# Two-layer graph attention on one core: feature-major head aggregation, pre-added softmax sums, second scores by dot products, deferred last aggregation

**Chip, cores, metric.** One NeuronCore of one Trainium2 chip. The metric is the device time of the whole program in microseconds (us), median of the timed runs. All runs quoted here agree within about 0.6% for one kernel and count as fast runs. In the profiles PE is TensorE, PEld its loading of stationary operands ("weight loads"), DVE is VectorE, ACT is ScalarE, POOL is GpSimd. The span goes from the first to the last instruction of the profiled run. The granted clock is the share of TensorE's full clock that it had in a stretch; 1.00 is full.

## The reference, cut to what matters

For each of 32 graphs (512 nodes, 512 features): layer norm and relu, a one-head graph attention with residual, then again layer norm and relu and a two-layer graph attention (4 heads of 256 features, then one head of 512).

```python
def gat_layer(x, mask, W, a_src, a_dst, bias, concat):
    xl = (x @ W).reshape(B, N, H, F)
    asrc = jnp.einsum('bnhf,hf->bnh', xl, a_src)
    adst = jnp.einsum('bnhf,hf->bnh', xl, a_dst)
    e = jax.nn.leaky_relu(asrc[:, :, None, :] + adst[:, None, :, :], NEG_SLOPE)
    e = jnp.where(mask[..., None], e, NEG_INF)
    attn = jax.nn.softmax(e, axis=1)
    out = jnp.einsum('bsdh,bshf->bdhf', attn, xl)
    ...                                         # concat or mean, + bias
h = jax.nn.elu(gat_layer(x, mask, W1, ..., concat=True))     # W1: 512 x 1024
h = gat_layer(h, mask, W2, ..., concat=False)                # W2: 1024 x 512
```

All of it is f32.

## The kernel before

T = 4 blocks of 128 nodes, H = 4 heads, F = 256, KH = 8 blocks of hidden features. E[s, d] are the softmax weights before division by their sum. The framework sets each engine's order of instructions when it builds the kernel; an engine then runs its stream in that order.

```python
def edge_weights(E, pq, h, a_of, a2_of, mask):
    p_row = spread(...); q_row = spread(...)            # TensorE: a value per node to a row
    for t in range(T):
        nc.scalar.activation(q, q_row, AF.Identity, bias=a2_of(t), scale=1.0)
        nc.vector.scalar_tensor_tensor(u, p_row, a_of(t), q, op0=ALU.add, op1=ALU.max)
        nc.gpsimd.tensor_add(u, u, mask[:, t, :])
        nc.scalar.activation(E[:, t, :], u, AF.Exp)

def inverse_sums(E):                                    # layer 0 and layer 2
    for t in range(T):
        for s in range(T):
            nc.tensor.matmul(ps[:, t:t+1], E[:, s, node_block(t)], ones, ...)
    nc.vector.reciprocal(r, ps)

def layer1_head(b, h, E):                               # nodes on the partitions
    for t in range(T):                                  # 257 columns: features and a column of ones
        acc = aggregate(E, t, lambda s: xl[:, s, h, :], F + 1)
        nc.vector.reciprocal(r[:, t:t+1], acc[:, F:F+1])
        nc.vector.scalar_tensor_tensor(v[:, t, :], acc[:, :F], r[:, t:t+1], b1_r[...], ...)
    ...                                                 # elu; later 8 transposes of v to h1T

def layer2_scores(b):
    ac, a2 = score_cols(H1T[b], wa2, 2, "2")            # 32 matmuls with 2 columns
    ...

# graph b:
layer1_project(b)
E = layer1_head_scores(b, 0)
for h in range(H):
    if more and h == 1:
        layer0_scores(b + 1); ...
    E_next = layer1_head_scores(b, h + 1) if h + 1 < H else None
    layer1_head(b, h, E); ...
if more: layer0_out(b + 1)
layer2_scores(b); layer2_project(b)
if more: layer1_in(b + 1)
layer2_out(b)
```

## Time and profile before

| | before |
|---|---|
| time, median of 2 | 5198.85 us (5193.39 to 5204.31) |
| span of the profiled run | 5205.4 us |
| TensorE busy / idle | 5003.1 / 202 us |
| granted TensorE clock, mean | 0.931 |
| one graph in the steady part | 160.4 us |

TensorE is the bound. The lines are in the prediction below. In the groups, the first number after the bar is busy time in us and the second the mean duration in ns; matmuls overlap one another, so busy time over count is the price on the line of time.

### The profile page before, as it was taken

To read this page: it belongs to the slowest core of one execution; us is meant where nothing else is said; L and a number is where in the kernel's file an instruction comes from. 1 tells how busy PE (TensorE), PEld (TensorE's weight loads), DVE (VectorE), ACT (ScalarE), POOL (GpSimd) and SP (SyncE) were. 2 spreads that over 40 slices of the span, in tenths; PEclk is the share of its full clock that TensorE was granted. 3 is DMA by queue.
4 is the path that set the end of the run, shared out by engine and by line. 5 is a ranking of instruction groups with operands and counts; after the bars stand their busy time and mean duration, and the time that the engine had idled before them with its cause. 6 is when DMAs were issued, how large, how long until landed. Compare 5 with 4: busy or idle time off the path is not lost.

```text
span 5205.4 us, 52686 instructions
## 1 busy us (share of the span) xinstructions
PE 5003.1 (96%) x20224; PEld 3228.5 (62%) x20224; DVE 2326.8 (45%) x6180; ACT 1794.5 (34%) x2945; POOL 1108.0 (21%) x998
## 2 busy tenths in 40 slices
PE   6999999999999999999999999999999999999999
PEld 3666656666566666666665666656666666666565
DVE  5454434454444544345443444444454434544343
ACT  2333323433224333233332333322433323333232
POOL 1222211222112212122221222211221212222121
PEclk8899999999999999999999999999999999999999
DMA  2000000000000000000000000000000000000000
GB/s 103 20 13 17 25 25 25 9 17 25 25 25 9 17 25 25 25 17 17 17 25 25 25 9 17 25 25 25 9 17 25 25 25 17 17 17 25 9 9 9
DMA packets 53802, 111.11 MB, mean 21 GB/s; under 512 B 1840, under 2 KB 1840, under 8 KB 53552
## 3 DMA queue, kind: packets, MB, share of 16 engines
q1 hardware_dynamic: 50688, 100.67, 5.5%
q10 hardware_dynamic: 2864, 7.08, 0.4%
q8 instruction: 160, 2.62, 0.2%
q14 instruction: 90, 0.74, 0.0%
HBM read 74.19 MB, written 33.55 MB: 21 GB/s over the span
## 4 chain that ended last, share of the span: by engine, by line
PE 86%; POOL 5%; DVE 5%; ACT 3%; issue 1%; DMA 1%; DVEq 0%; POOLq 0%; ACTq 0%; SPq 0%
PE acc L222 31%; PE acc L399 18%; PE acc L333 17%; PE ps_c L309 8%; POOL u L204 5%; PE row L165 4%; PE pt L173 3%; PE ps L212 3%; DVE u L203 3%; ACT q L201 2%; ACT E L205 1%; DVE v L367 1%; DMA x<-in_x_dram 0%; DVE junk L126 0%; DMA adj<-in_adj_dram 0%
## 5 line engine op out<-in xcount | busy, mean ns | idle before, releaser
L222 PE MATMUL acc<-xl,E 128*128 128x257 f32 (+1 forms) x5120 | 1548.6, 453 | 67.2 <-ACT E L205 62.1
L222 PEld LDWEIGHTS acc<-xl,E 128*128 128x128 f32 x5120 | 996.0, 203 | 470.4 <-issue 258.1
L204 POOL TENSOR_TENSOR u<-u,m 128x512 f32<-128x512 f32 x640 | 737.8, 1180 | 1844.2 <-DVE u L203 1803.7
L399 PE MATMUL acc<-w_s,h1T 128*128 128x512 f32 x2048 | 952.9, 619 | 0.0
L333 PE MATMUL acc<-w_s,hT 128*128 128x512 f32 x2048 | 917.3, 604 | 0.0
L203 DVE SCALAR_TENSOR_TENSOR u<-row,ac,q 128x512 f32<-128x512 f32 x640 | 447.5, 745 | 747.5 <-ACT q L201 746.1
L333 PEld LDWEIGHTS acc<-w_s,hT 128*128 128x128 f32 x2048 | 392.1, 196 | 449.8 <-issue 449.8
L399 PEld LDWEIGHTS acc<-w_s,h1T 128*128 128x128 f32 x2048 | 397.9, 201 | 436.7 <-issue 436.7
L201 ACT ACTIVATE q<-row,a 128x512 f32<-128x512 f32 x768 | 478.9, 682 | 535.2 <-PE row L165 428.4
L338 ACT COPY xl<-acc 128x512 f32<-128x512 f32 x256 | 150.1, 586 | 1340.7 <-PE acc L333 1340.7
L205 ACT ACTIVATE E<-u 128x512 f32<-128x512 f32 x768 | 484.2, 630 | 222.2 <-POOL u L204 221.2
L222 PE MATMUL acc<-h,E 128*128 128x512 f32 x1024 | 453.8, 601 | 6.0 <-DVE x L284 6.0
L180 DVE CUSTOM_DVE_ANT_0 junk_m<-m1T,row 128x512 bf16<-128x512 bf16 x640 | 394.4, 683 | 124.9 <-PE row L165 124.9
L309 PEld LDWEIGHTS ps_c<-wa,h1T 128*128 128x128 f32 x2048 | 335.4, 257 | 50.2 <-PE pt L173 34.1
L309 PE MATMUL ps_c<-wa,h1T 128*128 128x2 f32 x2048 | 333.1, 295 | 28.1 <-DVE r L216 28.1
L222 PEld LDWEIGHTS acc<-h,E 128*128 128x128 f32 x1024 | 194.7, 193 | 238.2 <-issue 224.1
L174 ACT COPY h1T<-pt 128x512 f32<-128x512 f32 x256 | 138.8, 581 | 551.3 <-PE pt L173 551.3
L411 DVE SCALAR_TENSOR_TENSOR x<-acc,r,x 128x512 f32<-128x512 f32 x128 | 96.1, 751 | 401.5 <-PE acc L222 401.5
L165 PE MATMUL row<-ident,pq 128*128 128x128 f32 x1536 | 210.6, 277 | 62.7 <-ACT q L201 53.3
L212 PEld LDWEIGHTS ps<-ones,E 128*128 128x128 f32 x2048 | 258.9, 198 | 11.2 <-ACT E L205 5.4
L212 PE MATMUL ps<-ones,E 128*128 128x1 f32 x2048 | 246.6, 246 | 4.4 <-ACT E L205 4.4
L165 PEld LDWEIGHTS row<-ident,pq 128*128 128x128 f32 x1536 | 175.3, 139 | 120.4 <-ACT q L201 71.1
(71 smaller groups left out, 3727.8 us busy)
## 6 DMA issues: line engine op xcount, KB each, us to landing
adj<-in_adj_dram SPq DMA_DIRECT2D x32, 1024.0 KB, 5.1
x<-in_x_dram SPq DMA_DIRECT2D x32, 1024.0 KB, 5.1
out_dram<-x SPq DMA_DIRECT2D x32, 1024.0 KB, 4.2
w_s<-in_L_gnn_W_dram ACTq DMA_DIRECT2D x2, 2048.0 KB, 21.1
b_r<-in_L_gnn_b_dram ACTq DMA_DIRECT2D x1, 512.0 KB, 11.2
a_r<-in_L_gnn_att_src_dram ACTq DMA_DIRECT2D x1, 512.0 KB, 5.4
a_r<-in_L_gnn_att_dst_dram ACTq DMA_DIRECT2D x1, 512.0 KB, 4.0
ws_r<-in_L_gnn_attn_w_src_dram ACTq DMA_DIRECT2D x1, 256.0 KB, 5.2
```

Of the source, the lines that this page charges most:

```text
L165: nc.tensor.transpose(row[:, node_block(t)], col_of(t).to_broadcast([P, P]), ident)
L173: nc.tensor.transpose(pt[:, node_block(t)], src(t, k), identity)
L180: nc.vector.tensor_tensor_reduce(junk, mask[:, t, :], row, 1.0, LOWEST, ALU.add, ALU.max, accum_out=amax[:, t, h : h + 1])
L201: nc.scalar.activation(q, q_row, AF.Identity, bias=a2_of(t), scale=1.0)
L203: nc.vector.scalar_tensor_tensor(u, p_row, a_of(t), q, op0=ALU.add, op1=ALU.max)
L204: nc.gpsimd.tensor_add(u, u, mask[:, t, :])
L205: nc.scalar.activation(E[:, t, :], u, AF.Exp)
L212: nc.tensor.matmul(ps[:, t : t + 1], E[:, s, node_block(t)], ones, start=(s == 0), stop=(s == T - 1))
L222: nc.tensor.matmul(acc[:, :width], E[:, s, node_block(t)], values(s), start=(s == 0), stop=(s == T - 1))
L309: nc.tensor.matmul(ps[:, t, :], src[:, k, node_block(t)], wa[:, k, :], start=(k == 0), stop=(k == kn - 1))
L333: nc.tensor.matmul(acc, hT[:, k, node_block(t)], w1_s[:, k, half * 512 : (half + 1) * 512], start=(k == 0), stop=(k == KD - 1),)
L399: nc.tensor.matmul(acc, h1T[:, k, node_block(t)], w2_s[:, k, :], start=(k == 0), stop=(k == KH - 1))
```

## The change

Its intent is to take work off TensorE: the head's output is made with features on the partitions (8 wide matmuls for 16 narrower ones, and no transposes), the softmax sums are pre-added on GpSimd so that 4 one-column matmuls do for 16, the second scores become dot products on VectorE, and the last aggregation of a graph moves behind the next graph's first projection. Core of the diff, cuts marked:

```diff
-    p_acc = ...(name="p_acc", bufs=2, space=PSUM)      # and p_tr bufs=2
+    p_acc = ...(name="p_acc", bufs=3, space=PSUM)      # and p_tr bufs=1
 ...
     def inverse_sums(E):
+        total = work.tile([P, N], F32, tag="total", name="total", bufs=1)
+        nc.gpsimd.tensor_add(total, E[0], E[1])
+        for e in E[2:]:
+            nc.gpsimd.tensor_add(total, total, e)
         for t in range(T):
-            for s in range(T):
-                nc.tensor.matmul(ps[:, t : t + 1], E[:, s, node_block(t)], ones, ...)
+            nc.tensor.matmul(ps[:, t : t + 1], total[:, node_block(t)], ones, start=True, stop=True)
 ...
     def layer1_head_scores(b: int, h: int):
-        return E
+        r = inverse_sums(E)
+        r_row = work.tile([P, N], F32, tag="r_row", ...)
+        nc.scalar.copy(r_row, spread(lambda t: r[:, t : t + 1]))
+        return E, r_row
 ...
+        for k in range(h * nk, (h + 1) * nk):           # layer1_head: features on the partitions
+            acc = aggregate_T(E, lambda s: xl[:, s, k * P : (k + 1) * P])
+            nc.vector.tensor_mul(v, acc, r_row)
+            nc.scalar.activation(e, v, AF.Exp, bias=bias, scale=1.0)
+            nc.vector.tensor_scalar(e, e, 1.0, -1.0, op0=ALU.min, op1=ALU.add)
+            nc.vector.scalar_tensor_tensor(H1T[b][:, k, :], v, bias, e, op0=ALU.add, op1=ALU.max)
 ...
+            for i in range(2):                          # layer2_project: scores 2
+                nc.vector.scalar_tensor_tensor(junk, xl[:, t, :], 1.0, att2_r[i], ..., accum_out=ac[:, t, i : i + 1])
 ...
-        E = layer1_head_scores(b, 0)
+        head = layer1_head_scores(b, 0)
+        if b:
+            layer2_out(b - 1)
 ...
+        layer2_project(b)
         layer2_scores(b)
-        layer2_project(b)
         if more:
             layer1_in(b + 1)
-        layer2_out(b)
```

More of the change, by code (lines that the diff above doesn't have):

```diff
@@ L71 @@
     cols = ctx.enter_context(tc.tile_pool(name="cols", bufs=2))
-    p_acc = ctx.enter_context(tc.tile_pool(name="p_acc", bufs=2, space=PSUM))
-    p_tr = ctx.enter_context(tc.tile_pool(name="p_tr", bufs=2, space=PSUM))
+    p_acc = ctx.enter_context(tc.tile_pool(name="p_acc", bufs=3, space=PSUM))
+    p_tr = ctx.enter_context(tc.tile_pool(name="p_tr", bufs=1, space=PSUM))
     p_bc = ctx.enter_context(tc.tile_pool(name="p_bc", bufs=3, space=PSUM))
@@ L107 @@
     nc.scalar.dma_start(w1_s, w1.rearrange("(k p) f -> p k f", p=P))
-    b1_r = const.tile([P, HF], F32, name="b1_r")
+    b1_c = const.tile([P, KH], F32, name="b1_c")
     b2_r = const.tile([P, D], F32, name="b2_r")
     wa1 = const.tile([P, KD, NW], F32, name="wa1")
-    wa2 = const.tile([P, KH, 2], F32, name="wa2")
+    att2_r = [const.tile([P, D], F32, name=f"att2_r{i}") for i in range(2)]
     def fold_attention_weights():
         nc.scalar.dma_start(w2_s, w2.rearrange("(k p) f -> p k f", p=P))
-        nc.scalar.dma_start(b1_r, rows(b1, HF))
+        with nc.allow_non_contiguous_dma(reason="one bias per partition"):
+            nc.scalar.dma_start(b1_c, b1.rearrange("(k p) -> p k", p=P))
         nc.scalar.dma_start(b2_r, rows(b2, D))
         for i, (a1, a2) in enumerate(((att_src1, att_src2), (att_dst1, att_dst2))):
-            a_r = work.tile([P, HF], F32, tag="v", name=f"a1_r{i}")
+            nc.scalar.dma_start(att2_r[i], rows(a2, D))
+            a_r = big.tile([P, HF], F32, tag="adj", name=f"a1_r{i}")
             nc.scalar.dma_start(a_r, rows(a1, HF))
@@ L124, in fold_attention_weights @@
                     f = slice(h * F, (h + 1) * F)
-                    junk = work.tile([P, D], F32, tag="junk", name="junk")
+                    junk = work.tile([P, D], BF16, tag="junk", name="junk")
                     nc.vector.scalar_tensor_tensor(
@@ L129, in fold_attention_weights @@
                     )
-            a_r = work.tile([P, D], F32, tag="v", name=f"a2_r{i}")
-            nc.scalar.dma_start(a_r, rows(a2, D))
-            for k in range(KH):
-                junk = work.tile([P, D], F32, tag="junk", name="junk")
-                nc.vector.scalar_tensor_tensor(
-                    junk, w2_s[:, k, :], 1.0, a_r, op0=ALU.mult, op1=ALU.mult,
-                    accum_out=wa2[:, k, i : i + 1],
-                )
     def node_block(t: int) -> slice:
@@ L193, in shifts, with edge_weights @@
         return pq
-    def edge_weights(E, pq, h, a_of, a2_of, mask):
+    def edge_weights(pq, h, a_of, a2_of, mask, name):
+        E = []
         p_row = spread(lambda t: pq[:, 0, t, h : h + 1])
@@ L199, in edge_weights @@
         for t in range(T):
-            q = work.tile([P, N], F32, tag="q", name="q", bufs=3)
-            nc.scalar.activation(q, q_row, AF.Identity, bias=a2_of(t), scale=1.0)
-            u = work.tile([P, N], F32, tag="u", name="u", bufs=4)
-            nc.vector.scalar_tensor_tensor(u, p_row, a_of(t), q, op0=ALU.add, op1=ALU.max)
+            u = work.tile([P, N], F32, tag="u", name="u", bufs=5)
+            nc.scalar.activation(u, q_row, AF.Identity, bias=a2_of(t), scale=1.0)
+            nc.vector.scalar_tensor_tensor(u, p_row, a_of(t), u, op0=ALU.add, op1=ALU.max)
             nc.gpsimd.tensor_add(u, u, mask[:, t, :])
-            nc.scalar.activation(E[:, t, :], u, AF.Exp)
+            e = big.tile([P, N], F32, tag="E", name=f"{name}_{t}", bufs=13)
+            nc.scalar.activation(e, u, AF.Exp)
+            E.append(e)
+        return E
     def inverse_sums(E):
+        total = work.tile([P, N], F32, tag="total", name="total", bufs=1)
+        nc.gpsimd.tensor_add(total, E[0], E[1])
+        for e in E[2:]:
+            nc.gpsimd.tensor_add(total, total, e)
         ps = p_sm.tile([P, T], F32, tag="sm", name="ps")
         for t in range(T):
-            for s in range(T):
-                nc.tensor.matmul(
-                    ps[:, t : t + 1], E[:, s, node_block(t)], ones, start=(s == 0), stop=(s == T - 1)
-                )
+            nc.tensor.matmul(ps[:, t : t + 1], total[:, node_block(t)], ones, start=True, stop=True)
         r = cols.tile([P, T], F32, name="r")
@@ L217, in inverse_sums, with aggregate, aggregate_T @@
         return r
-    def aggregate(E, t, values, width):
+    def aggregate(E, t, values):
         acc = p_acc.tile([P, 512], F32, tag="acc", name="acc")
         for s in range(T):
-            nc.tensor.matmul(
-                acc[:, :width], E[:, s, node_block(t)], values(s), start=(s == 0), stop=(s == T - 1)
-            )
+            nc.tensor.matmul(acc, E[s][:, node_block(t)], values(s), start=(s == 0), stop=(s == T - 1))
+        return acc
+    def aggregate_T(E, values):
+        acc = p_acc.tile([P, N], F32, tag="acc", name="acc_T")
+        for s in range(T):
+            nc.tensor.matmul(acc, values(s), E[s], start=(s == 0), stop=(s == T - 1))
         return acc
@@ L237, in masks @@
         nc.vector.tensor_scalar(m1, a, 0.0, NO_EDGE, op0=ALU.is_le, op1=ALU.mult)
-        d = cols.tile([P, T, P], F32, name="d")
+        d = work.tile([P, T, P], BF16, tag="junk", name="d")
         for t in range(T):
@@ L260, in layer0_scores @@
             for w, s in ((ws_r, c), (wd_r, a)):
-                junk = work.tile([P, D], F32, tag="junk", name="junk")
+                junk = work.tile([P, D], BF16, tag="junk", name="junk")
                 nc.vector.scalar_tensor_tensor(
@@ L272, in layer0_scores @@
         pq = shifts(c, amax, 1, "0")
-        E = big.tile([P, T, N], F32, tag="E0", name=f"E0_{b}")
-        edge_weights(E, pq, 0, lambda t: a[:, t, :], lambda t: a2[:, t, :], m0T)
+        E = edge_weights(pq, 0, lambda t: a[:, t, :], lambda t: a2[:, t, :], m0T, f"E0_{b}")
         L0[b] = (h0, E)
@@ L282, in layer0_out @@
         for t in range(T):
-            acc = aggregate(E, t, lambda s: h0[:, s, :], D)
+            acc = aggregate(E, t, lambda s: h0[:, s, :])
             nc.vector.scalar_tensor_tensor(
@@ L325, in layer1_project @@
         pq = shifts(ac[:, :, H:], amax, H, "1")
-        xl = big.tile([P, T, H, F + 1], F32, tag="xl", name=f"xl_{b}")
-        nc.gpsimd.memset(xl[:, :, :, F : F + 1], 1.0)
+        xl = big.tile([P, T, HF], F32, tag="xl", name=f"xl_{b}")
         for t in range(T):
@@ L336, in layer1_project @@
                     )
-                nh = 512 // F
-                nc.scalar.copy(
-                    xl[:, t, half * nh : (half + 1) * nh, :F], acc.rearrange("p (h f) -> p h f", f=F)
-                )
+                nc.scalar.copy(xl[:, t, half * 512 : (half + 1) * 512], acc)
         L1[b] = (ac, a2, pq, xl)
-    H1T, V1 = {}, {}
+    H1T = {}
     def layer1_head_scores(b: int, h: int):
         ac, a2, pq, _ = L1[b]
-        E = big.tile([P, T, N], F32, tag="E", name=f"E_{b}_{h}", bufs=2)
-        edge_weights(
-            E, pq, h, lambda t: ac[:, t, h : h + 1], lambda t: a2[:, t, h : h + 1], M[b][2]
-        )
-        return E
@@ L353, in layer1_head @@
-    def layer1_head(b: int, h: int, E):
-        xl = L1[b][3]
-        v = work.tile([P, T, F], F32, tag="v", name=f"v_{b}_{h}")
-        r = cols.tile([P, T], F32, name="r1")
-        for t in range(T):
-            acc = aggregate(E, t, lambda s: xl[:, s, h, :], F + 1)
-            nc.vector.reciprocal(r[:, t : t + 1], acc[:, F : F + 1])
-            nc.vector.scalar_tensor_tensor(
-                v[:, t, :], acc[:, :F], r[:, t : t + 1], b1_r[:, h * F : (h + 1) * F], op0=ALU.mult, op1=ALU.add
-            )
-        e = work.tile([P, T, F], F32, tag="e", name=f"e_{b}_{h}", bufs=1)
-        nc.vector.tensor_scalar(e, v, 0.0, None, op0=ALU.min)
-        nc.scalar.activation(e, e, AF.Exp)
-        nc.vector.scalar_tensor_tensor(v, e, -1.0, v, op0=ALU.add, op1=ALU.max)
-        V1[b, h] = v
@@ L370, in layer1_head_T, with layer1_head @@
-    def layer1_head_T(b: int, h: int):
+        E = edge_weights(
+            pq, h, lambda t: ac[:, t, h : h + 1], lambda t: a2[:, t, h : h + 1], M[b][2], f"E_{b}_{h}"
+        )
+        r = inverse_sums(E)
+        r_row = work.tile([P, N], F32, tag="r_row", name=f"r_row_{b}_{h}", bufs=1)
+        nc.scalar.copy(r_row, spread(lambda t: r[:, t : t + 1]))
+        return E, r_row
+    def layer1_head(b: int, h: int, E, r_row):
+        xl = L1[b][3]
         if h == 0:
             H1T[b] = big.tile([P, KH, N], F32, tag="h1T", name=f"h1T_{b}")
-        v = V1.pop((b, h))
@@ L374, in layer1_head_T @@
         nk = F // P
-        transposed(
-            lambda t, k: v[:, t, node_block(k)], H1T[b][:, h * nk : (h + 1) * nk, :], ident, F32
-        )
-    L2 = {}
-    def layer2_scores(b: int):
-        m1, m1T = M.pop(b)[2:]
-        L1.pop(b)
-        ac, a2 = score_cols(H1T[b], wa2, 2, "2")
-        amax = cols.tile([P, T, 1], F32, name="amax2")
-        neighbour_max(amax, 0, m1T, spread(lambda t: ac[:, t, 0:1]))
-        pq = shifts(ac[:, :, 1:2], amax, 1, "2")
-        E = big.tile([P, T, N], F32, tag="E", name=f"E_{b}_{H}", bufs=2)
-        edge_weights(E, pq, 0, lambda t: ac[:, t, 0:1], lambda t: a2[:, t, 0:1], m1)
-        L2[b] = E
+        for k in range(h * nk, (h + 1) * nk):
+            acc = aggregate_T(E, lambda s: xl[:, s, k * P : (k + 1) * P])
+            bias = b1_c[:, k : k + 1]
+            v = work.tile([P, N], F32, tag="v", name="v")
+            nc.vector.tensor_mul(v, acc, r_row)
+            e = work.tile([P, N], F32, tag="e", name="e")
+            nc.scalar.activation(e, v, AF.Exp, bias=bias, scale=1.0)
+            nc.vector.tensor_scalar(e, e, 1.0, -1.0, op0=ALU.min, op1=ALU.add)
+            nc.vector.scalar_tensor_tensor(H1T[b][:, k, :], v, bias, e, op0=ALU.add, op1=ALU.max)
@@ L393, in layer2_project @@
+    L2 = {}
     def layer2_project(b: int):
         h1T = H1T.pop(b)
-        xl = big.tile([P, T, D], F32, tag="xl", name=f"xl2_{b}")
+        xl = big.tile([P, T, D], F32, tag="xl2", name=f"xl2_{b}")
+        ac = cols.tile([P, T, 2], F32, name="ac2")
         for t in range(T):
@@ L402, in layer2_project, with layer2_scores @@
             nc.scalar.copy(xl[:, t, :], acc)
-        L2[b] = (L2[b], xl)
+            for i in range(2):
+                junk = work.tile([P, D], BF16, tag="junk", name="junk")
+                nc.vector.scalar_tensor_tensor(
+                    junk, xl[:, t, :], 1.0, att2_r[i], op0=ALU.mult, op1=ALU.mult, accum_out=ac[:, t, i : i + 1]
+                )
+        L2[b] = (ac, xl)
+    def layer2_scores(b: int):
+        m1, m1T = M.pop(b)[2:]
+        L1.pop(b)
+        ac, xl = L2[b]
+        a2 = cols.tile([P, T, 1], F32, name="a22")
+        nc.vector.tensor_scalar(a2, ac[:, :, 0:1], SLOPE, None, op0=ALU.mult)
+        amax = cols.tile([P, T, 1], F32, name="amax2")
+        neighbour_max(amax, 0, m1T, spread(lambda t: ac[:, t, 0:1]))
+        pq = shifts(ac[:, :, 1:2], amax, 1, "2")
+        E = edge_weights(pq, 0, lambda t: ac[:, t, 0:1], lambda t: a2[:, t, :], m1, f"E2_{b}")
+        L2[b] = (E, inverse_sums(E), xl)
     def layer2_out(b: int):
-        E, xl = L2.pop(b)
+        E, r, xl = L2.pop(b)
         xt = X.pop(b)
-        r = inverse_sums(E)
         for t in range(T):
-            acc = aggregate(E, t, lambda s: xl[:, s, :], D)
+            acc = aggregate(E, t, lambda s: xl[:, s, :])
             nc.vector.scalar_tensor_tensor(
@@ L431 @@
                     load(b + 2)
-            E_next = layer1_head_scores(b, h + 1) if h + 1 < H else None
-            layer1_head(b, h, E)
-            if h:
-                layer1_head_T(b, h - 1)
-            E = E_next
+            ahead = layer1_head_scores(b, h + 1) if h + 1 < H else None
+            layer1_head(b, h, *head)
+            head = ahead
         if more:
             layer0_out(b + 1)
-        layer1_head_T(b, H - 1)
+        layer2_project(b)
         layer2_scores(b)
-        layer2_project(b)
         if more:
             layer1_in(b + 1)
-        layer2_out(b)
+    layer2_out(B - 1)
 _INS = [
```

## The prediction

> **What bounds the kernel now.** I read the page's busy times first, then the chain that ended last, then the groups split by form, then TensorE's timeline of one steady graph, then the busy times by stretch.
>
> ```profile
> PE 5003.1 (96%) x20224; PEld 3228.5 (62%) x20224; DVE 2326.8 (45%) x6180; ACT 1794.5 (34%) x2945; POOL 1108.0 (21%) x998
> PE 86%; POOL 5%; DVE 5%; ACT 3%; issue 1%; DMA 1%; DVEq 0%; POOLq 0%; ACTq 0%; SPq 0%
> ```
>
> TensorE is busy 96% and makes 86% of the chain; no other engine reaches half. Idle time of TensorE is 5205 - 5003 = 202 us, 6 us in each of the 32 graphs. So time can only come from taking TensorE work away. Which work is there, and what does one instruction cost on the line of time (busy time over count, since the mean duration overlaps its neighbours)?
>
> ```profile
> L222 PE MATMUL acc<-xl,E 128*128 128x257 f32 x4096 | 1064.7, 408 | 67.2 <-ACT E L205 62.1 <-DVE v L361 1.7 <-DVE r L360 0.6
> L399 PE MATMUL acc<-w_s,h1T 128*128 128x512 f32 x2048 | 952.9, 619 | 0.0
> L309 PE MATMUL ps_c<-wa,h1T 128*128 128x2 f32 x2048 | 333.1, 295 | 28.1 <-DVE r L216 28.1
> L212 PE MATMUL ps<-ones,E 128*128 128x1 f32 x2048 | 246.6, 246 | 4.4 <-ACT E L205 4.4
> L165 PE MATMUL row<-ident,pq 128*128 128x128 f32 x1536 | 210.6, 277 | 62.7 <-ACT q L201 53.3 <-DVE pq L191 9.1
> L173 PE MATMUL pt<-ident,v 128*128 128x128 f32 x1024 | 137.9, 273 | 0.3 <-DVE v L367 0.3
> L204 POOL TENSOR_TENSOR u<-u,m 128x512 f32<-128x512 f32 x640 | 737.8, 1180 | 1844.2 <-DVE u L203 1803.7 <-DVE r L360 37.3
> ```
>
> The source asks for 32 x 32 matmuls in the second projection and the trace has 2048: each f32 matmul is two instructions, a transpose one. To be seen: the matmuls for the second scores have two columns and still cost 333.1/2048 = 163 ns each, the sums with one column 120 ns, against 465 ns for 512 columns. A narrow matmul pays for loading the 128 stationary columns.
>
> One graph lasts 2798.65 - 2638.25 = 160.4 us (between the same point of two graphs). The timeline around the second scores:
>
> ```profile
> 2757.56 0.73 PE L309 MATMUL ps_c<-wa,h1T 128*128 128x2 f32 x6
> 2758.15 1.11 PE L399 MATMUL acc<-w_s,h1T 128*128 128x512 f32 x2
> 2759.09 8.88 PE L309 MATMUL ps_c<-wa,h1T 128*128 128x2 f32 x52
> 2767.84 2.06 PE L399 MATMUL acc<-w_s,h1T 128*128 128x512 f32 x2
> 2769.69 1.06 PE L165 MATMUL row<-ident,ac 128*128 128x128 f32 x4
> 2770.54 4.20 PE L399 MATMUL acc<-w_s,h1T 128*128 128x512 f32 x8
> 2774.58 1.04 PE L165 MATMUL row<-ident,pq 128*128 128x128 f32 x8
> 2775.45 22.48 PE L399 MATMUL acc<-w_s,h1T 128*128 128x512 f32 x52
> ```
>
> Two things: some 10 us go to the narrow matmuls, and just after them two wide ones take 2.06 us, where 52 later ones take 22.48, so 0.43 us each. The stretches say why (columns: length, busy PE, PEld, DVE, ACT, POOL, granted clock, DMA):
>
> ```profile
> 2757.50:2767.80 10.30, 10.30 (x63) 9.82 (x61) 1.59 (x7) 3.83 (x6) 6.94 (x6) 0.69 0.01 2
> 2767.80:2797.80 30.00, 30.00 (x76) 14.11 (x77) 8.90 (x27) 6.58 (x11) 4.50 (x4) 0.93 0.10 35
> 2852.90:2903.30 50.40, 45.58 (x267) 38.36 (x266) 32.76 (x76) 33.85 (x57) 23.01 (x20) 0.97 0.00 1
> ```
>
> The granted clock falls to 0.69 under the narrow matmuls. The last row is the head stage, the one where the other engines are fullest: DVE 65%, ACT 67%, POOL 46%. Nearly all of TensorE's idle time is there.
>
> **What the Trainium skill says.** (1) "TensorE: Matmul & The Clock Gate", Part 1: the array's clock is halved after a window of about 3.4 us in which it was little used, and a matmul of 512 columns at full clock starts every 215.7 ns. The trace agrees on the clock (0.69, then two matmuls at twice their time); its f32 instruction takes 429 ns, twice the page's bf16 figure, with two instructions to a matmul. (2) "GPSIMD Engine Reference", section 3.1: an addition of two inputs takes about 2.6 cycles an element at 1.2 GHz. For 512 elements that is an estimate of 1109 ns; the trace has 1180 ns, and I use that. (3) The same page's specifications: GpSimd shares its SBUF interface with VectorE. The profile of before shows no clear slowing (1145 to 2141 ns for the mask additions, median 1157), so I add none. (4) "Perfetto Trace Analysis", Identifying the Most-Contended Engine: weight-load busy share judges TensorE better than matmul busy share. Here 62% against 96% says the same as the narrow matmuls: the array is occupied, not full.
>
> **The change part by part, on TensorE, for all 32 graphs.**
> 1. Heads with features on the partitions: per head 16 matmuls of 257 columns become 8 of 512. 4096 instructions at 260 ns (1064.7 us) become 2048. At the mean 455 ns of the four wide groups of today that is 932 us: -133. (In the densest stretch today's take 220 ns each, so a warm machine would give only some 20; most of this 133 is waiting and a cold clock inside the head stage.)
> 2. No more transposes of v, since the head's output comes out transposed: -138.
> 3. Second scores by dot products on VectorE: the 2048 two-column matmuls go: -333. VectorE gets 8 products a graph at the 0.69 + 0.08 us that the same form takes in layer 0: 6 us a graph, during the projection where it is busy 8.9 of 30 us. Hidden.
> 4. Sums pre-added on GpSimd: today 2 sets of 16 one-column matmuls a graph, then 6 sets of 4 (the heads need their own now, as the column of ones went). 2048 to 1536 instructions at 120 ns: -62. GpSimd gets 18 additions of 1.18 us a graph, 21 us.
> 5. The inverse sum must be spread to a row: 16 more transposes a graph, 512 at 137 to 200 ns: +80.
> 6. The clock after the second scores stays up: the second projection costs 952.9 us against 2048 x 0.429 = 879; I take 50 of the 74 us: -50.
> Sum: -133 - 138 - 333 - 62 + 80 - 50 = -636 us. From 5199 that is 4563.
>
> The other engines: GpSimd goes from 34.6 to about 56 us a graph, in the head stage from 23 to some 41 of about 65 us. VectorE: the head's five kinds of work today (reciprocals 79.9, scaling 242.6, minimum 101.8, maximum 157.9 us: 18.2 us a graph) become 8 products, 8 clampings and 8 maxima of 512, about 15; with the dot products it is 3 us more, 75 a graph. ScalarE stays near 56. None becomes the bound of a graph of 140 us.
>
> What is given back: the transposition pool has one PSUM buffer in place of two. The four groups of hn each need about 0.45 us of TensorE and then a copy of 0.59 us and two hand-overs; today the gaps are filled with the last aggregation's sums (the order in the timeline is hn, sums, hn, sums). Now little else is ready between the second projection and the next graph's first, because scores 2 only start when the projection ends: I estimate 3 us a graph, +96. The clock may fall again there (the 8-column scores follow): +15. The last graph has nothing to hide scores 2 behind: 4 dot-product ends, 4 maxima, 4 edge tiles at GpSimd's pace and 3 additions, about 15 us: +15. At the start the 16 products of the folded second weights (0.68 us) go: -10. In the head stage the sum of a head comes 3 x 1.18 = 3.5 us after its last weights; with one head of lead it should be hidden, and the deferred aggregation of 13.7 us fills the wait for head 0 (today 1.63 + 0.37 + 0.41 us idle); I leave these two against each other with 0. So 4563 + 116 = 4679; since the wide matmuls at 429 ns would take a further 50 us off step 1 if the stage ran without holes, I set 4650.
>
> As a check, the floor: 256 wide matmul instructions a graph of 429 ns = 110 us, and 25 us for scores 1, sums, spreads and transposes at today's warm rates: 135 us. With 80 us at the start and 145 for the last graph, 31 x 135 makes 4410. So 4650 holds 7 to 8 us of waiting a graph, against 4.8 to 6 now.
>
> **Rivals.**
> A. GpSimd's chain replaces TensorE in the head stage. Order on an engine is fixed, so if the sums' matmuls stand ahead of an aggregation in TensorE's stream and GpSimd is late, TensorE stops. For: 41 of 65 us of GpSimd in that stage, sums behind masks in one queue, and single buffers for total and the spread row. Against: TensorE's order today is visibly interleaved (transposes of masks between head matmuls), and the lead is a whole head of 7 us. It would add 3.5 us for each of 4 heads, 450 us: about 5100.
> B. Time comes back in full and the holes close: the deferred aggregation fills both the wait for head 0 and the hT gap, clock stays at 1.0: 4450 to 4500.
> C. The thirteen shared tiles for E: layer 0's four stay till the heads are done, so a head may wait for the head before the last to be aggregated. One tile more than today's twelve, freed singly, speaks against it; it would cost 2 to 4 us a graph, 4720 to 4780.
>
> **Range and chances.** Removals are counted instructions at measured prices and are sure within 15%; the waits are the uncertain term, between 3 and 13 us a graph. Predicted 4650 us, 8 in 10 between 4490 and 4820. Rival A in full still gives 2% less than today, so faster by over 2% is 0.95, within 2% 0.03, slower 0.02.
>
> **What would show it.** Right: no two-column matmuls and no transposes of v; head aggregation 2048 instructions near 910 to 930 us; the first matmuls of the second projection at 0.43 to 0.5 us; a graph of 140 to 145 us; a gap of about 3 us at the hn transposes released by ScalarE's copies; GpSimd near 1790 us. Wrong: TensorE idle over 400 us with releasers GpSimd or the sums' reciprocal (A); idle before edge weights released by TensorE through tile reuse (C); wide matmuls slower than 0.47 us each through the whole stage, which would be a lower granted clock.

## The result, and the profile after

The changed kernel takes 5832.51 us (5832.09 to 5832.94), the ratio to before is 1.1222 with a 95% interval of 1.1201 to 1.1243: 12% slower, where 11% faster was predicted. Ratios are the mean time of one kernel's fast runs over that of the other's of the same rounds, so not quite the ratio of the medians.

The page of the changed kernel: busy times, then the chain that ended last, by engine and by line.

```profile
PE 4989.9 (86%) x15104; PEld 2662.6 (46%) x15104; DVE 2741.3 (47%) x6244; ACT 1797.2 (31%) x2945; POOL 1894.2 (32%) x1542
...
PE 65%; POOL 22%; ACT 5%; issue 4%; DVE 3%; DMA 0%; DVEq 0%; ACTq 0%; POOLq 0%; SPq 0%
PE acc L380 15%; PE acc L221 13%; PE acc L334 12%; POOL u L198 12%; POOL total L209 8%; PE acc_T L228 8%; PE row L159 6%; PE ps L212 5%; PE ps_c L312 4%; DVE u L197 3%; ACT u L196 2%; PE pt L167 2%; POOL total L207 2%; ACT E L200 1%; ACT h L153 1%
```

TensorE has 5120 instructions fewer than before and is still busy 4990 us, as against 5003. It now idles 5830 - 4990 = 840 us in place of 202. In the chain GpSimd has 22% where it had 5%; it waits behind masks (L198) and additions of sums (L209, L207). The groups:

```profile
L228 PE MATMUL acc_T<-E,xl 128*128 128x512 f32 x2048 | 1164.0, 703 | 175.3 <-ACT E L200 175.2
L334 PE MATMUL acc<-w_s,hT 128*128 128x512 f32 x2048 | 1001.1, 634 | 0.0
...
L209 POOL TENSOR_TENSOR total<-total,E 128x512 f32<-128x512 f32 x384 | 560.1, 1458 | 19.0 <-ACT E L200 1.5
...
L212 PE MATMUL ps<-ones,total 128*128 128x1 f32 x1536 | 298.7, 316 | 569.9 <-POOL total L209 569.8
...
L312 PE MATMUL ps_c<-wa,hT 128*128 128x8 f32 x1024 | 215.9, 353 | 0.0
```

Two things are to be read. 570 us of TensorE's idle time stand ahead of the sums' matmuls, released by GpSimd's total, and 175 us ahead of the aggregations, released by edge weights (E). And wide matmuls have become dearer: 2048 instructions of one shape cost 1164 us in the heads and 1001 us in the first projection (917 before), where 2048 x 0.429 us = 879 us would do. Even the 8-column matmuls that the change does not touch went from 119.5 to 215.9 us. TensorE's timeline shows both things in one place (columns: start, length, engine, line, what, count, and the idle time before it):

```profile
2617.09 1.04 PE L159 MATMUL row<-ident,pq 128*128 128x128 f32 x8
2617.97 6.17 PE L221 MATMUL acc<-xl,E 128*128 128x512 f32 x14
2628.07 1.81 PE L212 MATMUL ps<-ones,total 128*128 128x1 f32 x8 [3.93 <-POOL total L209]
2629.74 2.05 PE L221 MATMUL acc<-xl,E 128*128 128x512 f32 x2
2631.59 1.06 PE L159 MATMUL row<-ident,r 128*128 128x128 f32 x4
2632.44 8.30 PE L221 MATMUL acc<-xl,E 128*128 128x512 f32 x16
```

The score rows of head 0 are done at 2617.97. Only 14 wide instructions (6.2 us, the last aggregation that was moved here) follow them in the stream, then the sums' matmuls. These need GpSimd's total, which comes at 2628.07. TensorE idles 3.93 us, and thereafter two wide instructions take 2.05 us, twice the usual. GpSimd in the same time:

```profile
2619.72 3.39 POOL L198 TENSOR_TENSOR u<-u,m 128x512 f32<-128x512 f32 x3 [34.60 <-DVE u L197]
2623.07 1.27 POOL L207 TENSOR_TENSOR total<-E,E 128x512 f32<-128x512 f32 x1
2624.30 1.15 POOL L198 TENSOR_TENSOR u<-u,m 128x512 f32<-128x512 f32 x1
2625.41 2.60 POOL L209 TENSOR_TENSOR total<-total,E 128x512 f32<-128x512 f32 x2
```

Seven operations one behind the other, 8.4 us, on top of a ScalarE and a VectorE step: the chain from rows to total lasts 10.1 us. The stretches tell the rest (length, busy time of PE, PEld, DVE, ACT, POOL, granted clock, DMA), of the changed kernel and, in the last line, of the 8-column matmuls in the kernel before:

```profile
2617.10:2624.10 7.00, 7.00 (x23) 3.34 (x21) 3.47 (x5) 4.91 (x8) 4.38 (x4) 1.00 0.29 111
2624.10:2628.10 4.00, 0.07 (x2) 0.03 (x1) 0.00 (x0) 0.63 (x1) 3.83 (x4) 1.00 0.00 0
2628.10:2632.40 4.30, 4.30 (x14) 3.16 (x15) 0.75 (x2) 0.00 (x0) 0.00 (x0) 0.51 0.00 0
...
2769.60:2776.30 6.70, 6.70 (x33) 6.66 (x32) 0.00 (x0) 0.59 (x1) 0.00 (x0) 0.50 0.00 0
...
2617.97:2798.87 180.90, 155.82 (x475) 83.41 (x473) 85.26 (x193) 56.10 (x92) 59.17 (x48) 0.86 0.05 17
```

```profile
2658.00:2661.50 3.50, 3.50 (x33) 3.43 (x31) 0.75 (x1) 0.00 (x0) 0.13 (x1) 1.00 0.44 167
```

The clock is at 1.00 up to the wait and at 0.51 after it. In the fourth row, the 32 untouched 8-column matmuls after layer 2's sums run at 0.50, 207 ns each (6.63 us for 32 in the chain), where before they ran at 1.00 and 108 ns (3.47 us for 32). The fifth row is one whole graph: 180.9 us at a mean clock of 0.86. Such a wait comes five times a graph (3.93, 3.64, 3.74 and 3.00 us for the heads, 4.09 us for layer 2), and besides one of 5.4 us for head 2's weights.

### The profile page after: what moved, and what is told of

It is laid out like the page before. It is cut to its first block, busy times and chain, and to the rows that moved or that the text cites. A ratio compares the mean times of both kernels' runs of the same rounds, so it can differ in the third digit from the quotient of the medians.

```text
span 5830.3 us, 43175 instructions
## 1 busy us (share of the span) xinstructions
PE 4989.9 (86%) x15104; PEld 2662.6 (46%) x15104; DVE 2741.3 (47%) x6244; ACT 1797.2 (31%) x2945; POOL 1894.2 (32%) x1542
## 4 chain that ended last, share of the span: by engine, by line
PE 65%; POOL 22%; ACT 5%; issue 4%; DVE 3%; DMA 0%; DVEq 0%; ACTq 0%; POOLq 0%; SPq 0%
PE acc L380 15%; PE acc L221 13%; PE acc L334 12%; POOL u L198 12%; POOL total L209 8%; PE acc_T L228 8%; PE row L159 6%; PE ps L212 5%; PE ps_c L312 4%; DVE u L197 3%; ACT u L196 2%; PE pt L167 2%; POOL total L207 2%; ACT E L200 1%; ACT h L153 1%
## 5 line engine op out<-in xcount | busy, mean ns | idle before, releaser
L198 POOL TENSOR_TENSOR u<-u,m 128x512 f32<-128x512 f32 x640 | 729.3, 1159 | 2734.8 <-DVE u L197 2734.8
L228 PE MATMUL acc_T<-E,xl 128*128 128x512 f32 x2048 | 1164.0, 703 | 175.3 <-ACT E L200 175.2
L380 PE MATMUL acc<-w_s,h1T 128*128 128x512 f32 x2048 | 884.1, 592 | 0.0
L212 PE MATMUL ps<-ones,total 128*128 128x1 f32 x1536 | 298.7, 316 | 569.9 <-POOL total L209 569.8
L197 DVE SCALAR_TENSOR_TENSOR u<-row,ac,u 128x512 f32<-128x512 f32 x640 | 442.1, 745 | 494.0 <-ACT u L196 493.2
L228 PEld LDWEIGHTS acc_T<-E,xl 128*128 128x128 f32 x2048 | 418.6, 226 | 531.1 <-issue 289.8
L212 PEld LDWEIGHTS ps<-ones,total 128*128 128x128 f32 x1536 | 288.1, 279 | 739.6 <-POOL total L209 724.8
L196 ACT ACTIVATE u<-row,a 128x512 f32<-128x512 f32 x768 | 471.3, 688 | 315.1 <-PE row L159 315.1
L209 POOL TENSOR_TENSOR total<-total,E 128x512 f32<-128x512 f32 x384 | 560.1, 1458 | 19.0 <-ACT E L200 1.5
L221 PE MATMUL acc<-xl,E 128*128 128x512 f32 x1024 | 527.4, 667 | 4.1 <-ACT E L200 4.1
L367 DVE TENSOR_SCALAR e<-e 128x512 f32<-128x512 f32 x256 | 226.1, 883 | 280.9 <-ACT e L366 280.9
L221 PEld LDWEIGHTS acc<-xl,E 128*128 128x128 f32 x1024 | 212.0, 217 | 230.0 <-issue 223.6
L198 POOL TENSOR_TENSOR u<-u,m0T 128x512 f32<-128x512 f32 x128 | 144.6, 1162 | 493.2 <-DVE u L197 493.2
```

What stands on the lines that cost most here:

```text
L196: nc.scalar.activation(u, q_row, AF.Identity, bias=a2_of(t), scale=1.0)
L197: nc.vector.scalar_tensor_tensor(u, p_row, a_of(t), u, op0=ALU.add, op1=ALU.max)
L209: nc.gpsimd.tensor_add(total, total, e)
L212: nc.tensor.matmul(ps[:, t : t + 1], total[:, node_block(t)], ones, start=True, stop=True)
L221: nc.tensor.matmul(acc, E[s][:, node_block(t)], values(s), start=(s == 0), stop=(s == T - 1))
L228: nc.tensor.matmul(acc, values(s), E[s], start=(s == 0), stop=(s == T - 1))
```

## The experiments

**Theory A**: TensorE's fixed stream has the sums' matmuls some 7 us behind the score rows, GpSimd's chain takes 10 us, so TensorE stands still; what is lost is a matter of placing, not of GpSimd's throughput. **Rival B**: GpSimd's work is itself the bound of the head stage. **Theory D**: a good part of the loss isn't the wait but the halved clock after it. Further rivals stand with the runs; the letters of this section are not those of the prediction. All runs gave a correct result unless said.

**1. Sums behind the aggregation.** The same instructions, written in another order:

```diff
-        r = inverse_sums(E)              # in layer1_head_scores, with r_row
-        return E, r_row
+        return (E,)
 ...                                      # in layer1_head:
+        accs = [aggregate_T(E, lambda s: xl[:, s, k * P : (k + 1) * P]) for k in ks]
+        r = inverse_sums(E)
+        r_row = ...; nc.scalar.copy(r_row, spread(...))
+        for k, acc in zip(ks, accs): ...
 ...                                      # in layer2_out:
+            if t == 0:
+                r = inverse_sums(E)
```

> The changed kernel with the sums (GpSimd additions, the four narrow matmuls, reciprocal, spread row) written after the head's aggregation instead of before it; same instructions. Theory A (TensorE stands still because the sums' matmuls lie only some 7 us of work behind the score rows in its fixed stream while GpSimd's chain takes 10 us, and the clock then halves): five stalls of 3.7 us and about 3 us of half clock after each go, 33 us of 181 a graph, so 4700 to 4900 us, clock 0.93 or more. Rival B (GpSimd and the supply of edge weights are the bound, the place of the sums doesn't matter): the idle time moves to the wait for edge weights, 5500 us or more, clock stays near 0.86.

Measured: 4878.17 us, ratio to before 0.9387 (0.9359 to 0.9415), clock 0.95. Theory A holds, rival B falls: GpSimd does 1844 us of work as against 1894, and the kernel is 954 us faster. TensorE's stream in one graph:

```profile
2501.28 1.04 PE L159 MATMUL row<-ident,pq 128*128 128x128 f32 x8
2502.15 3.60 PE L221 MATMUL acc<-xl,E 128*128 128x512 f32 x8
2505.59 0.95 PE L212 MATMUL ps<-ones,total 128*128 128x1 f32 x8
2506.40 10.55 PE L221 MATMUL acc<-xl,E 128*128 128x512 f32 x24
...
2544.92 2.08 PE L228 MATMUL acc_T<-E,xl 128*128 128x512 f32 x2 [3.72 <-ACT E L200]
```

The heads' and layer 2's sums now follow without idle time and the wide matmuls keep their 0.43 us; only layer 0's sums, which were not moved, still wait 1.9 us a graph. What is left besides is one large wait of 3.7 us for head 2's weights. This first mending beats the kernel before.

**2. Nobody waits for the total.** One operand:

```diff
-            nc.tensor.matmul(ps[:, t : t + 1], total[:, node_block(t)], ones, start=True, stop=True)
+            nc.tensor.matmul(ps[:, t : t + 1], E[t][:, node_block(t)], ones, start=True, stop=True)
```

> The changed kernel with the sums' matmuls reading the four weight tiles' diagonal blocks instead of the pre-added total (wrong result on purpose); the additions on GpSimd still run and nobody waits for them. Theory A: waits shrink to those for the weights and come in pieces of about 1 us, clock 0.93 or more, 4750 to 5050 us. Rival B: GpSimd does the same work, so 5500 us or more.

Measured: 5186.68 us, clock 0.926. Its output is wrong, which doesn't matter for the time. GpSimd's work is unchanged and 646 us go, so rival B falls again. It is over the top of what was expected of theory A: the large wait for head 2's weights (5.4 us) stays, and so do the 8-column matmuls at half clock. The stall is broken into pieces:

```profile
2502.78 3.60 PE L221 MATMUL acc<-xl,E 128*128 128x512 f32 x8
2506.40 0.38 PE L212 MATMUL ps<-ones,E 128*128 128x1 f32 x2
2506.64 1.10 PE L221 MATMUL acc<-xl,E 128*128 128x512 f32 x2
2507.58 0.31 PE L212 MATMUL ps<-ones,E 128*128 128x1 f32 x2
2508.63 0.38 PE L212 MATMUL ps<-ones,E 128*128 128x1 f32 x2 [0.73 <-ACT E L200]
```

Each sum waits for its own tile, 1.0 us at most for this head, and the wide matmuls between keep 1.10 us a pair.

**3. Pre-adding undone.** The sums as 16 one-column matmuls from the weights, in all six sets:

```diff
-        total = ...; nc.gpsimd.tensor_add(...)
-            nc.tensor.matmul(ps[:, t : t + 1], total[:, node_block(t)], ones, start=True, stop=True)
+            for s in range(T):
+                nc.tensor.matmul(ps[:, t : t + 1], E[s][:, node_block(t)], ones, ...)
```

> The changed kernel with the pre-adding undone: 16 narrow matmuls a set straight from the weights, six sets a graph. TensorE gets 12 x 8 x 0.11 = 16 us... worked out: 6 sets x 12 more matmuls x 2 instructions x 0.11 us = 16 us a graph more. Theory A: the stalls break into short waits for single weight tiles, the clock stays up, 33 us saved and 16 us spent: 5200 to 5400 us, faster than the changed kernel although TensorE does more. Rival C (the narrow matmuls themselves are what lowers the clock): slower than the changed kernel, over 5900 us.

Measured: 6021.83 us, clock 0.852. The expectation of theory A was wrong here, and the rival in the expectation had the sign. (Its 12 x 8 x 0.11 is a slip; the sum after it, 16 us, holds.) TensorE is busy 94% of the span: its idle time fell from 840 to 368 us, and its busy time rose from 4990 to 5652. The one-column matmuls, and two stretches (26 of them without a gap, and what comes after):

```profile
L209 PE MATMUL ps<-ones,E 128*128 128x1 f32 x6144 | 987.9, 284 | 281.0 <-ACT E L200 273.6
```

```profile
2712.60:2716.90 4.30, 4.30 (x27) 4.30 (x27) 0.00 (x0) 0.00 (x0) 0.00 (x0) 0.66 0.01 4
2716.90:2719.60 2.70, 2.70 (x7) 1.56 (x8) 0.18 (x1) 0.00 (x0) 0.00 (x0) 0.50 0.00 0
```

Within the run there is no idle time (4.30 of 4.30 us busy), and yet the granted clock is 0.66 over it and 0.50 after it. So the clock halved in a run of narrow matmuls, as it does after a wait. The price that I had used, 0.11 us, holds for a narrow matmul at full clock; here it was 988/6144 = 161 ns, and what followed paid too.

**4. Layer 0's scores after those of head 2** (early sums as in the changed kernel):

```diff
+            ahead = layer1_head_scores(b, h + 1) if h + 1 < H else None
             if more and h == 1:
                 layer0_scores(b + 1)
-            ahead = layer1_head_scores(b, h + 1) if h + 1 < H else None
```

> The changed kernel with one thing moved: the next graph's layer-0 scores are written after the scores of head 2 instead of before, sums still early. Theory A2 (the 5.4 us wait of a graph for head 2's weights comes from its score rows standing behind layer 0's): that wait goes, 32 x (5.4 + about 3 us of half clock) = 270 us less than the changed kernel, 5500 to 5650 us; the stalls at the sums stay, clock below 0.9. If the wait has another cause: within 60 us of 5830.

Measured: 5882.55 us. A miss: the wait did not go, it moved. It stands now ahead of head 3, as long as before:

```profile
2714.61 3.78 PE L228 MATMUL acc_T<-E,xl 128*128 128x512 f32 x4 [5.38 <-ACT E L200]
```

Whichever head's rows come behind layer 0's pays. Whether the row buffers or VectorE's maxima of layer 0 hold them up was not taken apart.

**5. Useless matmuls in the wait, and its control.** Four wide matmuls (8 instructions) as soon as GpSimd's first addition is there, for the heads and layer 2. To fit, the first addition has a tile of its own, the score buffers are 4 in place of 5, and the sums' PSUM tile is 512 columns wide; the control has these edits alone.

```diff
+        first = work.tile([P, N], F32, tag="first", name="first", bufs=1)
+        nc.gpsimd.tensor_add(first, E[0], E[1])
+        nc.gpsimd.tensor_add(total, first, E[2]); nc.gpsimd.tensor_add(total, total, E[3])
+        for _ in range(fill):                            # 4, in the control 0
+            nc.tensor.matmul(sm, ident, first, start=True, stop=True)
```

> The changed kernel with four useless wide matmuls (eight instructions, 3.4 us at full clock) before the sums' matmuls of the four heads and of layer 2, as soon as GpSimd's first addition is there; 17 us of work a graph more. Theory D (part of the loss is the clock, halved after a wait of TensorE of some 3.5 us, not the wait itself): the wait for GpSimd stays but is filled, clock rises from 0.86 to over 0.92, and the time falls by 100 to 350 us although TensorE does 550 us more: 5480 to 5730 us. If the clock follows nothing but the share of narrow matmuls, or the waits are all that is lost: 5850 us or more.

> Control of the run with useless matmuls: the same kernel with none of them (first addition into a tile of its own, four score buffers instead of five). Should be as the changed kernel: 5780 to 5880 us, clock 0.85 to 0.87. Outside of that, the fill run has to be compared with this one instead.

Measured: 5771.71 us at clock 0.939 with the filling, 5931.54 us at 0.855 without. The control fell outside its range (99 us slower than the changed kernel; which of its edits costs that was not taken apart), so the pair is compared with itself: the kernel that does more is 160 us faster. Busy times of the control, of the filled kernel, and the filling itself:

```profile
PE 5048.3 (85%) x15104; PEld 2692.4 (45%) x15104; DVE 2764.5 (47%) x6244; ACT 1793.8 (30%) x2945; POOL 1897.5 (32%) x1542
```

```profile
PE 5159.1 (89%) x16384; PEld 2585.7 (45%) x16384; DVE 2708.1 (47%) x6244; ACT 1794.1 (31%) x2945; POOL 1892.0 (33%) x1542
```

```profile
L213 PE MATMUL ps<-first,ident 128*128 128x512 f32 x1280 | 724.1, 718 | 301.6 <-POOL first L207 301.6
```

The filling costs 724 us of TensorE. The other 15104 instructions take 5159 - 724 = 4435 us, in the control 5048. So 613 us of the control's busy time went with the lower clock: the instructions are the same. Theory D holds. The time falls by less than that, since the 724 us of filling replace only some 270 us of idle time (882 in the control, 611 with the filling).

**6. Sums pre-added on VectorE.**

```diff
-        nc.gpsimd.tensor_add(total, E[0], E[1])          # and the loop
+        nc.vector.tensor_add(total, E[0], E[1])          # and the loop
```

> The changed kernel with the sums pre-added on VectorE instead of GpSimd; TensorE's order stays the same but for a place or two, the sums' matmuls still 8 wide matmuls behind the score rows. Theory A: masks on GpSimd no longer share it with sums, the chain from rows to total shrinks from 10 to some 7.5 us (0.7 + 0.8 + 4 x 1.16 + 0.6 + one addition), the stall from 3.7 to about 1 us, too short for the clock to fall: clock 0.92 or more, 5000 to 5350 us. Rival: VectorE, which has the larger load, delays the sums as much: 5600 us or more.

Measured: 5243.16 us, inside the expected range, but at clock 0.909, under the expected 0.92. The sums' matmuls stay where they were (8 wide matmuls behind the rows) and wait 242 us in place of 570; layer 2's still wait up to 2.60 us a graph. Of this kernel the sums' matmuls and two VectorE groups, then the same two groups of the changed kernel:

```profile
L212 PE MATMUL ps<-ones,total 128*128 128x1 f32 x1536 | 211.2, 259 | 242.3 <-DVE total L209 242.3
...
L368 DVE SCALAR_TENSOR_TENSOR h1T<-v,b_c,e 128x512 f32<-128x512 f32 x256 | 187.9, 744 | 4.5
...
L367 DVE TENSOR_SCALAR e<-e 128x512 f32<-128x512 f32 x256 | 108.9, 435 | 42.0 <-ACT e L366 42.0
```

```profile
L368 DVE SCALAR_TENSOR_TENSOR h1T<-v,b_c,e 128x512 f32<-128x512 f32 x256 | 278.1, 1086 | 8.9
...
L367 DVE TENSOR_SCALAR e<-e 128x512 f32<-128x512 f32 x256 | 226.1, 883 | 280.9 <-ACT e L366 280.9
```

VectorE got 18 additions a graph more and its own work became cheaper: the clamp 435 ns in place of 883, the maximum 744 in place of 1086. The mean of 883 mixes two kinds. Counted in the changed kernel's trace, 127 clamps that no GpSimd instruction overlaps in time take 427 ns, and 129 beside an addition into the total take 1332 ns. So it is not the additions as such but their falling together: run 1 has the same additions on GpSimd, at another time, and its mean clamp takes 448 ns.

**7. Second scores by narrow matmuls again**, in the kernel of run 1:

```diff
-            nc.vector.scalar_tensor_tensor(junk, xl[:, t, :], 1.0, att2_r[i], ..., accum_out=ac[:, t, i : i + 1])
+        ac, a2 = score_cols(H1T[b], wa2, 2, "2")         # scores before the projection, as before
```

> The late-sums kernel with the second scores by 64 two-column matmul instructions a graph again instead of dot products. If the price in the prediction's step 3 and 6 holds (333 + 50 us over the run) this is 380 us slower than the late-sums kernel's 4878 us: 5200 to 5300 us, and the clock falls in that stretch. If scores 2 starting before the projection give some of it back: 5000 to 5150 us.

Measured: 5242.33 us, 364 us over run 1's 4878.17. The prediction had 333 + 50 = 383 us for this part: right to 5%.

**8. All mended.** Run 1, and layer 0's scores in head 2's turn behind those of head 3, and layer 0's sums after its second aggregation:

```diff
-            if more and h == 1:                          # ahead of the next head's scores
+            if more and h == 2:                          # behind them
 ...
-        r = inverse_sums(E)                              # layer0_out
+            if t == 1:
+                r = inverse_sums(E)
```

> Sums after the aggregation as in the late-sums run, and layer-0 scores moved to head 2's turn after the scores of head 3, and layer 0's own sums after its second aggregation. Theory A with A2: no wait of TensorE over 2 us is left in the head stage, clock 0.97 or more, a graph of 138 to 143 us, 4480 to 4680 us. Rival B (with the order mended GpSimd's or VectorE's work in the head stage binds): about 4800 to 4880 us, idle before the aggregations released by the weights.

Measured: 4708.05 us, ratio to before 0.9071 (0.9058 to 0.9085), clock 0.969: 9.3% faster than before, 19% faster than the change as it came, and with run 9 the fastest of all, though a little over the expected range. Busy times, two groups, one graph:

```profile
PE 4405.0 (94%) x15104; PEld 2289.2 (49%) x15104; DVE 2620.9 (56%) x6244; ACT 1786.7 (38%) x2945; POOL 1870.0 (40%) x1542
```

```profile
L228 PE MATMUL acc_T<-E,xl 128*128 128x512 f32 x2048 | 1035.1, 641 | 39.0 <-DVE v L368 37.5 <-ACT E L200 1.5
...
L212 PE MATMUL ps<-ones,total 128*128 128x1 f32 x1536 | 182.2, 240 | 0.8 <-POOL total L209 0.8
```

```profile
2559.17:2699.00 139.83, 132.25 (x460) 69.31 (x459) 81.36 (x193) 55.22 (x91) 58.44 (x48) 0.96 0.05 16
```

The waits of the heads for sums (0.8 us in the whole run) and for weights (1.5 us) are gone. A graph takes 139.8 us. Of the 300 us still idle, 79 stand ahead of mask transposes, which wait for ScalarE to empty the one transposition buffer, and 61 and 38 ahead of the rows and products of late sums. A second transposition buffer was not tried.

**9. The last part of it taken back.** Layer 0's sums ahead of its first aggregation again:

```diff
+        r = inverse_sums(E)                              # layer0_out
-            if t == 1:
-                r = inverse_sums(E)
```

> The 4708 us version without its last part: layer 0's sums stand before its first aggregation again. They lie about 5 us behind layer 0's score rows, the chain is 10 us: a stall of 3 to 5 us a graph and half clock after it, 4820 to 4960 us. If the sums are ready by then: 4700 to 4740 us.

Measured: 4707.53 us, the same. The expected stall was a miss, the alternative right: these sums were ready in time, and that edit is worth nothing.

**10. Deferral undone**, in the kernel of run 8:

```diff
-        if b:
-            layer2_out(b - 1)                            # behind head 0's scores
 ...
         if more:
             layer1_in(b + 1)
+        layer2_out(b)
```

> The best version so far (4708 us) with the last aggregation put back before the next graph's first projection. If the deferral hides scores 2: TensorE waits some 12 us a graph for the maximum and the weights of layer 2, and some 4 us for head 0's weights, plus half clock after both: 5150 to 5400 us. If other work fills these holes: under 4850 us.

Measured: 5205.57 us, 498 us slower than run 8, as expected: TensorE's idle time is 584 us in place of 300, and its busy time 4621 in place of 4405. So the deferral hides what the dot products have made late. The largest hole of a graph is shorter than the 12 us expected. It stands between the last score rows of layer 2 and its aggregation:

```profile
2624.25 1.97 PE L159 MATMUL row<-ident,pq 128*128 128x128 f32 x8 [0.19 <-DVE pq L185]
2629.68 6.68 PE L221 MATMUL acc<-xl,E 128*128 128x512 f32 x10 [3.46 <-ACT E L200]
```

## Why the prediction was wrong

By its own steps:

- **What is taken off TensorE.** Right in sum where the clock holds, but not in each step. The steps predicted a busy time of 5003 - 636 = 4367 us; run 8, which does the change's TensorE work, has 4405. Second scores and projection together were right to 5% (run 7), the transposes of v are gone, the second projection fell from 952.9 to 884.1 us (69 us, predicted 50). The sums were predicted at 185 us and are 182 in run 8, but 299 in the changed kernel; the spread rows at 80 and are 85, but 134. Step 1 was mis-sized: the heads were to fall by 133 us to 932 and fell by 30 to 1035 in run 8 (1164 in the changed kernel), near the "some 20" that the step gives in brackets. That the sum still came out is partly luck: groups that no step names fell too, layer 2's aggregation from 484 to 455 us, the rows of layer scores from 138.5 to 102, while the first projection rose from 917 to 953. What the changed kernel has over run 8 goes with the lower clock; the filling of run 5 brings heads, sums and spread rows to 1008, 191 and 77.
- **The hn transposes with one PSUM buffer, +96 us.** Wrong, too dear: all idle time ahead of them is 6.5 us in the changed kernel. The next graph's first projection filled the gaps (its wide matmuls stand between the transposes in the timeline).

```profile
L167 PE MATMUL pt<-ident,hn 128*128 128x128 f32 x512 | 81.3, 281 | 6.5 <-ACT hn L153 5.8 <-ACT hT L168 0.7
```

- **The step that failed** is the one on the head stage: the sum of a head "should be hidden" with one head of lead, "and the deferred aggregation of 13.7 us fills the wait for head 0 [...] I leave these two against each other with 0". The lead in the stream was 6.2 us of wide matmuls for head 0 and 7.0 for head 1 and layer 2, over half of the deferred aggregation (18 of 32 instructions) stood behind the sums instead of ahead, and the chain was 10.1 us. In place of 0 the sums cost 570 us of waiting, and the clock fell after it. Of the 1180 us by which the prediction missed, some 560 are idle time (840 us, where 4650 - 4367 = 283 were implied) and some 620 busy time (4990 in place of 4367).
- **Rival A** named the mechanism and set it at 3.5 us for each of 4 heads, about 5100 us. The waits were five a graph, not four, since layer 2's sums stall as well, and they were 3.0 to 4.1 us; that was sized fairly. What it left out is the clock. Between the changed kernel and run 8 a graph differs by 180.9 - 139.8 = 41.1 us: idle time 25.1 against 7.6, so 17.5 us of waiting, and busy time 155.8 against 132.3, so 23.5 us for the same matmuls. The greater half was busy time at a lower clock (0.86 against 0.96), and the prediction itself had shown that clock falling under narrow matmuls.
- **The argument against A** was that the lead is "a whole head of 7 us". I never added up the chain that it has to cover: 0.7 + 0.8 us of ScalarE and VectorE, 4 masks and 3 additions on GpSimd, 10 us.
- **GpSimd's price.** Predicted 1790 us busy, measured 1894. The price of 1180 ns was read off mask additions, whose second input is bf16; of the additions for sums, which read two f32 tiles, the 229 that no VectorE instruction overlaps take 1268 ns in the changed kernel's trace, and the 189 beside VectorE's maximum 1521. So the base price was too low, and the contention that I took as 0 from the trace of before is there. VectorE had 85.3 us of work a graph in place of the predicted 75.
- **Rival C** (tiles for E): a wait for head 2's weights exists, 175 us in all, but run 4 shows it moving with the place of layer 0's rows and run 8 shows it gone with the same 13 tiles. Which resource holds the rows up stays open.

The direction of the whole was not an error of the idea: with the same arithmetic on the same engines, placed otherwise, it is 9.3% faster than before.

## What to carry to other kernels

When a new producer is put ahead of an instruction of the bounding engine, add up the whole chain up to that producer and compare it with the work that stands between in the bounding engine's stream; being a loop turn ahead says nothing until both sums are made. Put the consumer as late as its own consumers allow: here the sums are not needed until the aggregation is done. On TensorE, price a wait of some 3 us, or as long a run of narrow matmuls, at its own length and half speed for what follows: after head 0's wait of 3.93 us the clock stood at 0.50 for nearly 7 us, and after layer 2's of 4.09 us, with 32 narrow matmuls behind it, for 17.

## What the Trainium skill lacked or had wrong

- "TensorE: Matmul & The Clock Gate", Part 1 and "Why this matters for your kernels": the advice is to avoid idle gaps of more than about 3 us. The runs agree for waits of 3.6 to 4.1 us (clock 0.50 after them), but show two things more. Shorter waits next to narrow matmuls were followed by half speed too: in one graph of run 6, 2.60 us ahead of layer 2's sums (then a wide pair in 2.05 us) and 1.18 us ahead of head 0's (then four wide ones in 3.48 us), while after 1.37 us ahead of head 3's a pair took 1.10; no threshold comes out of these runs. And narrow matmuls without a gap do it too: 0.66 over 26 one-column instructions, 0.50 after (run 3). They are no small matter at half clock: the 8-column matmuls took 108 ns each at 1.00 and 207 ns at 0.50.
- "GPSIMD Engine Reference", section 1: it names contention with VectorE, without a size. Here VectorE's clamp took 1332 ns in the mean where an addition on GpSimd overlapped it and 427 where nothing did, and GpSimd's additions for sums took 1521 ns beside VectorE's maximum and 1268 beside nothing.
